# Attention with its scores in a ring of three pairs of PSUM banks and its spread reciprocals in SBUF

## The chip, the core and the metric

The kernel runs on one core of a Trainium2 chip. The core has five engines that work side by side and meet through semaphores: TensorE (PE in the profile, its weight loads PEld), VectorE (DVE), ScalarE (ACT), GpSimd (POOL) and SyncE (SP, which issues most of the DMAs here). The metric is the device time of one execution in microseconds; the median of several executions is compared.

## What is computed

The program is two layers of a MetaFormer on x of 8 images, 128 channels, 32 by 32 pixels. Layer 0 is an attention mixer followed by a spectral mixer; layer 1 is a deformable convolution followed by a mixture of eight experts. The change lies in the attention alone:

```
xp = transpose(ln(x), (0, 2, 3, 1))                  # b, h, w, c
q, k, v = (xp @ w.T).reshape(b, h, w, 8, 16)         # 8 heads of 16 channels
weights = einsum('bhwnd,bxynd->bnhwxy', q, k) / 4
weights = softmax(weights, axis=-1)                  # over y: groups of 32 keys
attn = einsum('bnhwxy,bxynd->bhwnd', weights, v)
x = x + transpose(attn.reshape(b, h, w, c), (0, 3, 1, 2))
```

The softmax runs over the last axis only. A query pixel therefore has 32 separate softmaxes per head, one for each row x of keys, each over 32 keys, and the 32 weighted sums are added.

## The kernel before

All numbers are float32. The attention that runs is `attention_bounded` (the other branch is taken only for inputs whose scores could overflow). It works in **rounds**. An image has 1024 tokens. A **unit** is one block of 256 queries (`QU`, index `qc`) and one half of the heads (`hg`, four heads), so an image has 8 units and the eight images have 64. A unit takes four rounds `r`, and each round covers two of the eight tiles of 128 keys (`c`), for four heads `j`: 256 rounds in all.

- `scores` (L596) makes 8 matmuls into the tile `s` of four PSUM banks, with four heads in four row tiles of 32 rows of the PE array; each head has its 16 channels there and 16 rows of zeros. Then ACT takes one exponential of 2048 elements per partition into `e` in SBUF (L609). `s` has one buffer.
- `add_tiles` (L615): POOL adds the two key tiles of `e` into `t` (L618), 1024 elements per partition from two inputs in SBUF.
- `sums` (L621): PE adds groups of four partitions of `t` into `z`; with the layout of the keys that completes the 32 keys of a softmax. All four rounds of a unit are summed in one round.
- `reciprocals` (L630): DVE takes the reciprocal of `z` out of PSUM into `r`.
- `spread_out` (L634): PE spreads `r` back over the partitions into `rb`, two PSUM banks.
- `divide` (L644): DVE multiplies `e` by `rb` in place (L646), 2048 elements per partition; one input is in SBUF, the other, `rb`, in PSUM.
- `values` (L650): PE multiplies `e` with the values into `av`, one bank, over both halves of the heads.
- `take` and `results` (L664, L668): ACT copies `av` to `o`, PE turns it round with the selection matrix `pick` (L673), which also puts the channels in order, ACT copies it to `at`, and POOL adds it to the image's tokens `xt`.

In between lie the projections for the next image: `keys` (L569) once for each half of the heads and half of the tokens, `queries` (L555), `key_values` (L582), the transposes `tokens` and `channels`, and the layer norm in small pieces on DVE (`bn_stats`, `bn_aggr`), POOL (a row of short operations on 8 elements, L87 to L99) and ACT.

PSUM has eight banks. Before the change four are `s`, two `rb`, one `av`, and one (`small_bank`) is shared by `z` and all projections.

Every engine executes its instructions in program order. That order is written out by hand: `at(round, order, step)` collects all steps, and they are issued sorted by round and by the order within it, with semaphores where tiles are shared. In round R the scores of round R come first (order 0), then POOL's add (1), then `values` of an older unit (2), `spread_out` (2.5), one `divide` (3), `sums` (4), `reciprocals` (5), and the projections (5.5, 6). `e` has 11 buffers, so that it may live from its exponential to its `values`.

Of the kernel before, what the change touches and what calls it, by code (L numbers as in the profile page):

```python
# [11 lines left out]
F32 = mybir.dt.float32  # L12
I32 = mybir.dt.int32
AF = mybir.ActivationFunctionType
ALU = mybir.AluOpType
AX = mybir.AxisListType
PSUM = bass.MemoryType.PSUM

P = 128
B = 8  # L20
C = 128
# [378 lines left out]
class BoundedAttention:  # L400
# [6 lines left out]
    def __init__(self, nc, cp):  # L407
        self.nc = nc
        HG, NH = self.HG, self.NH
        self.xc = cp.tile([P, T], F32, name="xc")  # L410
        self.ht = cp.tile([P, NT, C], F32, name="ht")
        self.hk = cp.tile([P, T], F32, name="hk")
        self.wq, self.wk = (cp.tile([P, HG, NH, 32], F32, name=n) for n in ("wq", "wk"))
        self.wv = cp.tile([C, C], F32, name="wv")
        self.group = cp.tile([P, NG], F32, name="group")
        self.spread = cp.tile([P, 2, P], F32, name="spread")
        self.pick = cp.tile([P, HG, NH, HD], F32, name="pick")

    def keys_view(self):
        return self.hk.rearrange("c (r p) -> c r p", p=P)  # L420
# [34 lines left out]

    def matrices(self, wqT, wkT, wvT):
        nc, HG, NH = self.nc, self.HG, self.NH
        for w, src in ((self.wk, wkT), (self.wq, wqT)):
            nc.gpsimd.memset(w, 0.0)
            for hg in range(HG):  # L460
                nc.sync.dma_start(
                    w[:, hg, :, 0:HD],
                    src[:, hg * NH * HD : (hg + 1) * NH * HD].rearrange("c (h d) -> c h d", d=HD),
                )
        nc.sync.dma_start(self.wv, wvT)

        group = self.group
        nc.gpsimd.memset(group, 1.0)
        nc.gpsimd.affine_select(
            out=group, in_=group, pattern=[[-4, NG]], base=0, channel_multiplier=1,  # L470
            compare_op=ALU.is_ge, fill=0.0,
        )
        nc.gpsimd.affine_select(
            out=group, in_=group, pattern=[[4, NG]], base=3, channel_multiplier=-1,
            compare_op=ALU.is_ge, fill=0.0,
        )

        nc.gpsimd.memset(self.spread, 0.0)
        for j in range(NH):
            part = self.spread[32 * j : 32 * j + 32, j % 2, :].rearrange("p (g m) -> p g m", m=4)  # L480
            nc.gpsimd.affine_select(
                out=part, in_=part, pattern=[[-1, NG], [0, 4]], base=0, channel_multiplier=1,
                compare_op=ALU.not_equal, fill=1.0,
            )


        nc.gpsimd.memset(self.pick, 0.0)
        for hg in range(HG):
            nc.gpsimd.affine_select(
                out=self.pick[:, hg], in_=self.pick[:, hg], pattern=[[-32, NH], [-1, HD]],  # L490
                base=-HD * hg, channel_multiplier=1, compare_op=ALU.not_equal, fill=1.0,
            )


def attention_bounded(ctx, tc, ident, x, x1d, given, weigh, head):


# [8 lines left out]
    QU = 256  # L506
    QC = T // QU
    UNITS = HG * QC
    wq, wk, wv = given.wq, given.wk, given.wv
    group, spread, pick = given.group, given.spread, given.pick  # L510
    hk = given.keys_view()
    cp = ctx.enter_context(tc.tile_pool(name="a_const", bufs=1))
    sb = ctx.enter_context(tc.tile_pool(name="a_sb", bufs=2))
    ep = ctx.enter_context(tc.tile_pool(name="a_e", bufs=11))
    sp = ctx.enter_context(tc.tile_pool(name="a_s", bufs=1, space=PSUM))
    rp = ctx.enter_context(tc.tile_pool(name="a_r", bufs=1, space=PSUM))


# [47 lines left out]
            pq.rearrange("p (r g m) -> p r g m", r=4, m=4),  # L566
        )

    def keys(img, hg, par):  # L569
        if "k" not in img:  # L570
            img["k"] = sb.tile([P, HG, NT, P], F32, tag="k", name="k")
        pk = small_bank("pk")
        nc.tensor.matmul(  # L573
            pk, wk[:, hg].rearrange("c h d -> c (h d)"),
            hk[:, 4 * par : 4 * par + 4, :].rearrange("c r p -> c (r p)"),
            start=True, stop=True,
        )
        nc.scalar.copy(
            img["k"][:, hg, 4 * par : 4 * par + 4, :].rearrange("p c n -> p (c n)"), pk
        )  # L580

    def key_values(b, img, par):  # L582
# [13 lines left out]
    def scores(img, un, r):  # L596

        qc, hg = un["at"]
        s = sp.tile([P, NH, 2, QU], F32, tag="s", name="s")
        q = img["q"][:, hg].rearrange("p a t -> p (a t)")  # L600
        for c in range(2):
            for j in range(NH):
                rows = slice(32 * j, 32 * j + 32)
                nc.tensor.matmul(  # L604
                    s[:, j, c, :], img["k"][rows, hg, 2 * r + c, :],
                    q[rows, qc * QU : (qc + 1) * QU], start=True, stop=True,
                )
        e = ep.tile([P, NH, 2, QU], F32, tag="e", name="e")
        nc.scalar.activation(  # L609
            e.rearrange("p j c q -> p (j c q)"), s.rearrange("p j c q -> p (j c q)"), AF.Exp,  # L610
            scale=float(HD) ** -0.5,
        )
        un["e", r] = e

    def add_tiles(un, r):  # L615
# [16 lines left out]
        nc.vector.reciprocal(un["r"], un["z"][:, 0:QU])  # L632

    def spread_out(un):  # L634
        un["rb"] = rp.tile([P, NH, QU], F32, tag="rb", name="rb")
        for h in range(2):
            for pr in range(2):
                rows = slice(64 * pr, 64 * pr + 64)
                nc.tensor.matmul(  # L639
                    un["rb"][:, 2 * pr + h, :], spread[rows, h, :], un["r"][rows, :],  # L640
                    start=True, stop=True,
                )

    def divide(un, r):  # L644
        e = un["e", r]
# [22 lines left out]
    def results(b, img, qc, qrt):  # L668
        if qc == 0:
            img["at"] = sb.tile([P, NT, C], F32, tag="at", name="at", bufs=1)  # L670
        po = small_bank("po")
        for i in range(2):
            nc.tensor.matmul(  # L673
                po[:, i * P : (i + 1) * P], qrt["o"][:, i * P : (i + 1) * P],
                pick.rearrange("p g j d -> p (g j d)"), start=True, stop=True,
            )
        nc.scalar.copy(
            img["at"][:, 2 * qc : 2 * qc + 2, :].rearrange("p i c -> p (i c)"), po[:, 0 : 2 * P]
        )
        mine = [img[n][:, 2 * qc : 2 * qc + 2, :] for n in ("xt", "at")]  # L680
        nc.gpsimd.tensor_add(mine[0], mine[0], mine[1])
        if qc == QC - 1:
            nc.sync.dma_start(x1d[b], img["xt"])
# [4 lines left out]
    def at(round_no, order, do, *args):  # L688
        work.append((round_no, order, len(work), do, args))
# [5 lines left out]
    for b in range(B):  # L695
        img = {}
        first = 4 * UNITS * b
        project = [
            (keys, img, 0, 0), (keys, img, 0, 1), (queries, img, 0, 0),
            (keys, img, 1, 0), (keys, img, 1, 1), (queries, img, 1, 0),  # L700
            (key_values, b, img, 0), (key_values, b, img, 1),
            (queries, img, 0, 1), (queries, img, 1, 1),
        ]
        if b == 0:
            turn = {"tokens": (0, 0)}
            project_at = (-1, -1, -1, 0, 1, 2, 3, 4, 7, 11)
        else:
            project_at = [first + n for n in (-13, -12, -9, -5, -4, -1, 3, 4, 7, 11)]
            turn = {"channels": (first - 20, first - 17)}
            if b == 1:  # L710
                turn.update(load=0, tokens=(2, 3))
                norm_at = (3, 3, 4, 4, 5, 5, 6, 6) + (6, 7, 7, 8, 8, 8, 9, 9, 9) + (
                    10, 10, 10, 11, 13, 13, 14, 14)
            else:
                turn.update(load=first - 42, tokens=(first - 38, first - 34))
                norm_at = [first - n for n in (
                    37, 36, 35, 34, 33, 32, 32, 31, *range(31, 22, -1), 22, 22, 22, 21, 19, 19, 18, 18
                )]
# [13 lines left out]
        for qc in range(QC):  # L732
            qrt = {}
            for hg in range(HG):
                un = {"at": (qc, hg)}
                t0 = first + 4 * (HG * qc + hg)
                for r in range(4):
                    at(t0 + r, 0, scores, img, un, r)
                    at(t0 + r, 1, add_tiles, un, r)
                    at(t0 + 5, 4, sums, un, r)  # L740
                    at(t0 + 6 + r, 3, divide, un, r)
                at(t0 + 8, 2, values, img, un, 0, (0, 1), qrt)
                at(t0 + 8, 6.5, values, img, un, 1, (0,), qrt)
                at(t0 + 9, 2, values, img, un, 1, (1,), qrt)
                at(t0 + 10, 2, values, img, un, 2, (0, 1), qrt)
                at(t0 + 11, 2, values, img, un, 3, (0, 1), qrt)
                at(t0 + 5, 5, reciprocals, un)
                at(t0 + 6, 2.5, spread_out, un)
            at(t0 + 11, 5, take, qrt)
            at(t0 + 12, 6, results, b, img, qc, qrt)  # L750
    end = 4 * UNITS * B
    spread_rounds(head.pieces(), (end - 40, *range(end - 30, end)))
    with tc.manual_schedule(engines=None):
# [1486 lines left out]
```

## Time and profile before

| | us |
|---|---|
| median of 3 runs | 1885.28 (1880.29 to 1889.61) |
| the profiled execution, its own time | 1886.46 |
| its span, first to last instruction | 1884.7 |
| first exponential of the attention starts | 32.3 |
| last exponential ends | 888.7 |
| granted TensorE clock, whole span / 102 to 850 us / 896 to 1884 us | 0.959 / 1.00 / 0.92 |

| engine | busy in the span, us | busy from 102 to 850 us (748 us), us |
|---|---|---|
| PE | 1682.4 | 742.61 |
| DVE | 1389.0 | 618.25 |
| POOL | 1157.9 | 576.73 |
| ACT | 1064.8 | 507.68 |

The stretch from 102 to 850 us is the attention in its steady course; 225 of the 256 rounds start their exponential in it. A group row of the profile gives the line, the engine, the operation, output and inputs by the program's names, the shapes, the number of instructions, then their busy time and the mean duration in ns, and last the idle time of the engine just before them with what ended it. In a timeline the first number is the start and the second the duration, in us. A PE that is busy all the time is not necessarily at its peak, since matmuls overlap.

### The profile page before, as it was taken

Reading aid. Unit: us, or ns where it says so; the run is one execution under the profiler, and the core shown is the slowest. Engines: PE = TensorE matmul, PEld = TensorE weight load, DVE = VectorE, ACT = ScalarE, POOL = GpSimd, SP = SyncE. Lnnn points to the kernel's source line nnn. Section 1 sums busy time; section 2 is a strip of 40 time slices with the busy share of each in tenths; the row PEclk is TensorE's granted clock in tenths of the full one; section 3 lists DMA queues with packets and bytes.
Section 4 is the critical chain, followed back from the end, with each engine's and each line's share of the span. In section 5 each row is a group of like instructions: output and inputs, shape, how many; then the busy total and the mean of one; then the engine's idle time right before and its main releaser. Section 6 shows DMA issues by size and latency. Waiting matters only on the chain.

```text
span 1884.7 us, 51873 instructions
## 1 busy us (share of the span) xinstructions
PE 1682.4 (89%) x22324; PEld 1033.1 (55%) x22324; DVE 1389.0 (74%) x2107; ACT 1064.8 (56%) x1692; POOL 1157.9 (61%) x1219
## 2 busy tenths in 40 slices
PE   6899999999999999998577899999888497888788
PEld 3455555555555555554233688888665264555555
DVE  3688787878888888888544666666148888999883
ACT  3666666676766667666234455555145655666630
POOL 3778777777878777787221244345126768888740
PEclk9999999999999999999788999999899687999999
DMA  1000000000000000000658322122568775755620
GB/s 30 13 2 24 2 2 24 2 24 2 24 2 24 2 2 24 2 13 2 143 142 242 129 71 71 48 71 59 179 194 263 237 213 153 234 174 164 205 81 21
DMA packets 157998, 156.15 MB, mean 83 GB/s; under 512 B 15424, under 2 KB 136864, under 8 KB 156352
## 3 DMA queue, kind: packets, MB, share of 16 engines
q1 hardware_dynamic: 142400, 102.41, 19.1%
q0 software_dynamic: 15360, 50.34, 8.5%
q8 instruction: 176, 2.88, 0.6%
q14 instruction: 62, 0.51, 0.1%
HBM read 96.39 MB, written 56.33 MB: 81 GB/s over the span
## 4 chain that ended last, share of the span: by engine, by line
PE 60%; DVE 16%; issue 7%; POOL 6%; ACT 4%; DMA 2%; SPq 2%; DVEq 0%; ACTq 0%; POOLq 0%
PE s L604 14%; PE av L656 13%; PE p_g L1958 6%; PE z L625 6%; PE p_z L2007 5%; PE rb L639 4%; PE p_out L1420 3%; DVE ga L1410 3%; DVE g L1317 2%; ACT e L609 2%; PE pq L559 2%; PE pk L573 2%; POOL g L1295 1%; DVE zs L2019 1%; PE po L673 1%
## 5 line engine op out<-in xcount | busy, mean ns | idle before, releaser
L618 POOL TENSOR_TENSOR t<-e 128x1024 f32<-128x1024 f32 x256 | 608.2, 2376 | 204.7 <-ACT e L609 204.4
L646 DVE TENSOR_TENSOR e<-e,rb 128x2048 f32<-128x2048 f32 x256 | 570.4, 2278 | 84.5 <-PE rb L639 84.5
L609 ACT ACTIVATE e<-s 128x2048 f32<-128x2048 f32 x256 | 481.0, 1879 | 255.1 <-PE s L604 252.0
L604 PE MATMUL s<-q,k 32*128 32x256 f32 x4096 | 295.2, 402 | 14.6 <-ACT e L609 13.8
L656 PE MATMUL av<-e,vt 128*32 128x256 f32 x4096 | 287.4, 388 | 4.8 <-DVE e L646 3.5
L1295 POOL DMA_INDIRECT g<-tab,idx x192 | 200.3, 1043 | 134.1 <-ACT cn_m L1515 66.8
L604 PEld LDWEIGHTS s<-q,k 32*128 32x128 f32 x4096 | 185.9, 185 | 137.8 <-ACT e L609 116.9
L1302 ACT ACTIVATE g<-g,w 128x128 f32<-128x128 f32 x604 | 186.4, 390 | 57.0 <-DMA g<-tab,idx 43.2
L1983 POOL TENSOR_SCALAR at<-uc 128x256 f32<-128x256 f32 (+2 forms) x62 | 75.4, 1219 | 173.4 <-PE p_z L2007 128.9
L656 PEld LDWEIGHTS av<-e,vt 128*32 128x32 f32 x4096 | 101.1, 109 | 141.5 <-issue 83.8
L1958 PE MATMUL p_g<-v,a 32*128 32x128 f32 x4096 | 159.3, 284 | 9.4 <-ACT ga L1690 3.7
L632 DVE RECIPROCAL r<-z 128x256 f32<-128x256 f32 x64 | 112.5, 1758 | 70.4 <-PE z L625 70.2
L1958 PEld LDWEIGHTS p_g<-v,a 32*128 32x128 f32 x4096 | 132.3, 186 | 38.3 <-issue 23.0
L1420 PE MATMUL p_out<-ga,ew 128*128 128x512 f32 x256 | 127.5, 645 | 15.5 <-DVE ga L1410 15.4
L625 PE MATMUL z<-t,group 128*32 128x256 f32 x2048 | 122.2, 379 | 0.0
L1692 DVE COPY gb<-p_g 128x512 f32<-128x512 f32 x128 | 82.4, 685 | 46.7 <-PE p_g L1958 46.1
L1692 DVE COPY ga<-p_g 128x512 f32<-128x512 f32 x128 | 82.4, 686 | 44.0 <-PE p_g L1958 44.0
L1690 ACT COPY gb<-p_g 128x512 f32<-128x512 f32 x128 | 68.7, 589 | 69.6 <-PE p_g L1958 68.8
L1690 ACT COPY ga<-p_g 128x512 f32<-128x512 f32 x128 | 68.7, 589 | 66.7 <-PE p_g L1958 66.7
L1410 DVE TENSOR_TENSOR ga<-p_g,tc 128x2048 f32<-128x2048 f32 x32 | 73.0, 2282 | 29.5 <-PE p_g L1401 29.5
L1420 PEld LDWEIGHTS p_out<-ga,ew 128*128 128x128 f32 x256 | 50.1, 205 | 75.6 <-issue 56.2
L625 PEld LDWEIGHTS z<-t,group 128*32 128x32 f32 x2048 | 66.4, 110 | 44.1 <-issue 0.3
(312 smaller groups left out, 2421.3 us busy)
## 6 DMA issues: line engine op xcount, KB each, us to landing
tab<-hx SPq DMA_DIRECT2D x24, 512.0 KB, 5.8
tab<-hx SPq DMA_DIRECT2D x72, 128.0 KB, 5.3
ud<-us SPq DMA_DIRECT2D x8, 1024.0 KB, 5.3
uc<-ud SPq DMA_DIRECT2D x16, 512.0 KB, 4.0
yd<-zs SPq DMA_DIRECT2D x32, 256.0 KB, 3.2
ga<-yd SPq DMA_DIRECT2D x32, 256.0 KB, 3.8
xc<-in_x SPq DMA_DIRECT2D x8, 512.0 KB, 3.9
x1d<-xt SPq DMA_DIRECT2D x8, 512.0 KB, 2.9
```

The source lines that it names most:

```text
L604: nc.tensor.matmul(s[:, j, c, :], img["k"][rows, hg, 2 * r + c, :], q[rows, qc * QU : (qc + 1) * QU], start=True, stop=True,)
L609: nc.scalar.activation(e.rearrange("p j c q -> p (j c q)"), s.rearrange("p j c q -> p (j c q)"), AF.Exp, scale=float(HD) ** -0.5,)
L618: nc.gpsimd.tensor_add(t, e[:, :, 0, :], e[:, :, 1, :])
L625: nc.tensor.matmul(un["z"][32 * j : 32 * j + 32, 0:QU], group, un["t", r][:, j, :], start=(r == 0), stop=(r == 3), skip_group_check=True,)
L646: nc.vector.tensor_tensor(e, e, un["rb"].unsqueeze(2).to_broadcast([P, NH, 2, QU]), ALU.mult)
L656: nc.tensor.matmul(qrt["av"][32 * j : 32 * j + 32, 0:QU], img["v"][:, 2 * r + c, P * hg + 32 * j : P * hg + 32 * j + 32], un["e", r][:, j, ...
L1295: nc.gpsimd.indirect_dma_start(out=t["g", i][:, tap].rearrange("p k c -> p (k c)"), out_offset=None, in_=rows, in_offset=bass.IndirectOffs ...
L1302: nc.scalar.activation(t["g", i][:, tap, k, :], t["g", i][:, tap, k, :], AF.Identity, scale=t["w"][:, i, tap, k : k + 1],)
L1420: nc.tensor.matmul(t["out"], self.ew[:, first + e, :], xg[:, e, :], start=(first + e == 0), stop=(first + e == NE - 1), skip_group_check=True,
L1690: self.nc.scalar.copy(dst, src)
L1692: self.nc.vector.tensor_copy(dst, src)
L1958: nc.tensor.matmul(banks[j][:, i * P : (i + 1) * P], self.a[rows, 4 * n + i, :], self.v[rows, ch].rearrange("p f k -> p (f k)"), start=Tru ...
```

## The change

There are five edits.

1. **Ring.** The score tile becomes two tiles of two banks each, out of a pool of three such pairs. A round takes two pairs; the exponential becomes two instructions of 1024 elements, one for each pair.
2. **Spread reciprocals.** `rb` no longer has banks of its own. `spread_out` writes into a pair of the ring, ACT copies that to a new SBUF tile `rbs`, and `divide` reads both of its inputs, `e` and `rb`, from SBUF. PSUM is then six banks of ring, one of `av`, one shared.
3. **Keys.** Two heads share a row tile of keys: rows 0 to 15 and 16 to 31 of a row tile hold the keys of heads 2j and 2j+1, and the queries have zeros in the rows of the other head. `keys` runs once per half of the tokens, not once per half of the heads too. The weight tiles are loaded accordingly: one DMA for `wk`, two each for `wq` and `wv`, five as before.
4. **Results.** The heads come out in the order of the channels, so `pick` goes and its matmul becomes a transpose.
5. **Order.** `divide`, `values` and `take` come one round later, `results` two rounds later, and the projections follow the shorter list.

```diff
         self.hk = cp.tile([P, T], F32, name="hk")
-        self.wq, self.wk = (cp.tile([P, HG, NH, 32], F32, name=n) for n in ("wq", "wk"))
-        self.wv = cp.tile([C, C], F32, name="wv")
+        self.wq = cp.tile([P, HG, NH, 32], F32, name="wq")
+        self.wk = cp.tile([C, C], F32, name="wk")
+        self.wv = cp.tile([C, HG, NH, HD], F32, name="wv")
         self.group = cp.tile([P, NG], F32, name="group")
         self.spread = cp.tile([P, 2, P], F32, name="spread")
-        self.pick = cp.tile([P, HG, NH, HD], F32, name="pick")
...
         nc, HG, NH = self.nc, self.HG, self.NH
-        for w, src in ((self.wk, wkT), (self.wq, wqT)):
-            nc.gpsimd.memset(w, 0.0)
-            for hg in range(HG):
-                nc.sync.dma_start(
-                    w[:, hg, :, 0:HD],
-                    src[:, hg * NH * HD : (hg + 1) * NH * HD].rearrange("c (h d) -> c h d", d=HD),
-                )
-        nc.sync.dma_start(self.wv, wvT)
+        nc.sync.dma_start(self.wk, wkT)
+        nc.gpsimd.memset(self.wq, 0.0)
+        for hg in range(HG):
+            at = slice(HD * hg, HD * hg + HD)
+            nc.sync.dma_start(
+                self.wq[:, hg, :, at], wqT.rearrange("c (h n) -> c h n", n=2 * HD)[:, :, at]
+            )
+            nc.sync.dma_start(
+                self.wv[:, hg], wvT.rearrange("c (h n) -> c h n", n=2 * HD)[:, :, at]
+            )
...
-        nc.gpsimd.memset(self.pick, 0.0)
-        for hg in range(HG):
-            nc.gpsimd.affine_select(
-                out=self.pick[:, hg], in_=self.pick[:, hg], pattern=[[-32, NH], [-1, HD]],
-                base=-HD * hg, channel_multiplier=1, compare_op=ALU.not_equal, fill=1.0,
-            )
-
-
 def attention_bounded(ctx, tc, ident, x, x1d, given, weigh, head):
...
     UNITS = HG * QC
-    wq, wk, wv = given.wq, given.wk, given.wv
-    group, spread, pick = given.group, given.spread, given.pick
+    wq, wk, wv = given.wq, given.wk, given.wv.rearrange("c g j d -> c (g j d)")
+    group, spread = given.group, given.spread
     hk = given.keys_view()
...
     ep = ctx.enter_context(tc.tile_pool(name="a_e", bufs=11))
-    sp = ctx.enter_context(tc.tile_pool(name="a_s", bufs=1, space=PSUM))
+    sp = ctx.enter_context(tc.tile_pool(name="a_s", bufs=3, space=PSUM))
     rp = ctx.enter_context(tc.tile_pool(name="a_r", bufs=1, space=PSUM))
...
-    def keys(img, hg, par):
+    def keys(img, par):
         if "k" not in img:
-            img["k"] = sb.tile([P, HG, NT, P], F32, tag="k", name="k")
+            img["k"] = sb.tile([P, NT, P], F32, tag="k", name="k")
         pk = small_bank("pk")
         nc.tensor.matmul(
-            pk, wk[:, hg].rearrange("c h d -> c (h d)"),
-            hk[:, 4 * par : 4 * par + 4, :].rearrange("c r p -> c (r p)"),
+            pk, wk, hk[:, 4 * par : 4 * par + 4, :].rearrange("c r p -> c (r p)"),
             start=True, stop=True,
...
         nc.scalar.copy(
-            img["k"][:, hg, 4 * par : 4 * par + 4, :].rearrange("p c n -> p (c n)"), pk
+            img["k"][:, 4 * par : 4 * par + 4, :].rearrange("p c n -> p (c n)"), pk
         )
...
         qc, hg = un["at"]
-        s = sp.tile([P, NH, 2, QU], F32, tag="s", name="s")
+        s = [sp.tile([P, 2, 2, QU], F32, tag="s", name="s") for _ in range(2)]
         q = img["q"][:, hg].rearrange("p a t -> p (a t)")
...
                 nc.tensor.matmul(
-                    s[:, j, c, :], img["k"][rows, hg, 2 * r + c, :],
+                    s[j // 2][:, j % 2, c, :], img["k"][rows, 2 * r + c, :],
                     q[rows, qc * QU : (qc + 1) * QU], start=True, stop=True,
...
         e = ep.tile([P, NH, 2, QU], F32, tag="e", name="e")
-        nc.scalar.activation(
-            e.rearrange("p j c q -> p (j c q)"), s.rearrange("p j c q -> p (j c q)"), AF.Exp,
-            scale=float(HD) ** -0.5,
-        )
+        for h in range(2):
+            nc.scalar.activation(
+                e[:, 2 * h : 2 * h + 2].rearrange("p j c q -> p (j c q)"),
+                s[h].rearrange("p j c q -> p (j c q)"), AF.Exp, scale=float(HD) ** -0.5,
+            )
         un["e", r] = e
...
     def spread_out(un):
-        un["rb"] = rp.tile([P, NH, QU], F32, tag="rb", name="rb")
+        rb = sp.tile([P, 2, 2, QU], F32, tag="s", name="rb")
         for h in range(2):
...
                 nc.tensor.matmul(
-                    un["rb"][:, 2 * pr + h, :], spread[rows, h, :], un["r"][rows, :],
-                    start=True, stop=True,
-                )
+                    rb[:, pr, h, :], spread[rows, h, :], un["r"][rows, :], start=True, stop=True,
+                )
+        un["rb"] = sb.tile([P, NH, QU], F32, tag="rbs", name="rbs")
+        nc.scalar.copy(
+            un["rb"].rearrange("p j q -> p (j q)"), rb.rearrange("p a h q -> p (a h q)")
+        )
...
         for i in range(2):
-            nc.tensor.matmul(
-                po[:, i * P : (i + 1) * P], qrt["o"][:, i * P : (i + 1) * P],
-                pick.rearrange("p g j d -> p (g j d)"), start=True, stop=True,
+            nc.tensor.transpose(
+                po[:, i * P : (i + 1) * P], qrt["o"][:, i * P : (i + 1) * P], ident
             )
...
         project = [
-            (keys, img, 0, 0), (keys, img, 0, 1), (queries, img, 0, 0),
-            (keys, img, 1, 0), (keys, img, 1, 1), (queries, img, 1, 0),
+            (keys, img, 0), (keys, img, 1), (queries, img, 0, 0), (queries, img, 1, 0),
             (key_values, b, img, 0), (key_values, b, img, 1),
...
             turn = {"tokens": (0, 0)}
-            project_at = (-1, -1, -1, 0, 1, 2, 3, 4, 7, 11)
+            project_at = (-1, -1, -1, 2, 3, 4, 7, 11)
         else:
-            project_at = [first + n for n in (-13, -12, -9, -5, -4, -1, 3, 4, 7, 11)]
+            project_at = [first + n for n in (-13, -12, -9, -1, 3, 4, 7, 11)]
             turn = {"channels": (first - 20, first - 17)}
...
                     at(t0 + 5, 4, sums, un, r)
-                    at(t0 + 6 + r, 3, divide, un, r)
-                at(t0 + 8, 2, values, img, un, 0, (0, 1), qrt)
-                at(t0 + 8, 6.5, values, img, un, 1, (0,), qrt)
-                at(t0 + 9, 2, values, img, un, 1, (1,), qrt)
-                at(t0 + 10, 2, values, img, un, 2, (0, 1), qrt)
-                at(t0 + 11, 2, values, img, un, 3, (0, 1), qrt)
+                    at(t0 + 7 + r, 3, divide, un, r)
+                at(t0 + 9, 2, values, img, un, 0, (0, 1), qrt)
+                at(t0 + 9, 6.5, values, img, un, 1, (0,), qrt)
+                at(t0 + 10, 2, values, img, un, 1, (1,), qrt)
+                at(t0 + 11, 2, values, img, un, 2, (0, 1), qrt)
+                at(t0 + 12, 2, values, img, un, 3, (0, 1), qrt)
                 at(t0 + 5, 5, reciprocals, un)
                 at(t0 + 6, 2.5, spread_out, un)
-            at(t0 + 11, 5, take, qrt)
-            at(t0 + 12, 6, results, b, img, qc, qrt)
+            at(t0 + 12, 5, take, qrt)
+            at(t0 + 14, 6, results, b, img, qc, qrt)
     end = 4 * UNITS * B
...
     with tc.manual_schedule(engines=None):
...
```

## The prediction

> **What bounds the kernel now.** I read the page first, for the share of each engine, then the attention's steady stretch, 102 to 850 us, in the table of windows, the groups and the chain. The page's groups for the attention:
>
> ```profile
> L618 POOL TENSOR_TENSOR t<-e 128x1024 f32<-128x1024 f32 x256 | 608.2, 2376 | 204.7 <-ACT e L609 204.4
> L646 DVE TENSOR_TENSOR e<-e,rb 128x2048 f32<-128x2048 f32 x256 | 570.4, 2278 | 84.5 <-PE rb L639 84.5
> L609 ACT ACTIVATE e<-s 128x2048 f32<-128x2048 f32 x256 | 481.0, 1879 | 255.1 <-PE s L604 252.0
> ```
>
> Each of the three runs once a round. The stretch holds 225 exponentials in 748 us, so a round takes 3.324 us and a unit of four 13.30 us; 748 us are 56.25 units. No engine of the three needs that long. The chain of waits over the stretch names the one that does:
>
> ```profile
> by line: PE s L604 33.0%; PE av L656 29.9%; PE z L625 12.9%; PE rb L639 8.0%; PE pq L559 4.0%; PE pk L573 4.0%; PE po L673 2.4%; ACT e L609 2.3%; PE pv L585 2.0%; PE pt L539 1.1%; PE pb L547 0.5%; issue 0.1%
> ```
>
> All but 2.4% is PE. The exponential lies on it with 2.3%: the places where PE is ready for the next scores before `s` is free. Per unit the engines are busy (the stretch's sums over 56.25): PE 13.2 us, DVE 618.25/56.25 = 11.0, POOL 576.73/56.25 = 10.3, ACT 507.68/56.25 = 9.0. DVE and POOL together would need 21.3 us; they fit in 13.3 only because they overlap. Whether they still can is the question that decides here.
>
> [...] `divide` reads `e` from SBUF and `rb` from PSUM, and in the stretch its 226 executions, nearly all beside a POOL addition, hardly vary (minimum, median, maximum in ns):
>
> ```profile
> L646 DVE TENSOR_TENSOR e<-e,rb x226: 2252/2280/2291, 102.2 to 849.4; 128x2048 f32<-128x2048 f32 x113
> ```
>
> Layer 1 has DVE instructions with both inputs in SBUF. L1317 takes 0.95 us as a rule. Once (first two rows) POOL's addition starts 0.07 us before it, once (last two) DVE is first by 0.16 us:
>
> ```profile
> 1428.95 2.37 POOL L1221 TENSOR_TENSOR tok<-tok,cb 128x1024 f32<-128x1024 f32 x1
> 1429.02 3.13 DVE L1317 TENSOR_TENSOR g<-g 128x768 f32<-128x768 f32 x1
> ...
> 1458.01 0.94 DVE L1317 TENSOR_TENSOR g<-g 128x768 f32<-128x768 f32 x1
> 1458.17 3.00 POOL L1221 TENSOR_TENSOR tok<-tok,cb 128x1024 f32<-128x1024 f32 x1 [2.44 <-DVE ht L1076]
> ```
>
> In the first case POOL ends at 1431.32 and DVE at 1432.15: DVE did 0.83 of its 0.95 us after POOL's end, so 0.12 overlapped. In the second DVE ends at 1458.95, POOL at 1461.17: 2.22 of its 2.37 us came after, so 0.15 overlapped. That is full exclusion, with only the start of an instruction hidden.
>
> [...] I keep 2.278 us for its own work (no row of before shows the SBUF form at this size; the 0.95 us of 768 elements plus 1280 elements at the slope 2278/2048 gives 2.37, the other end).
>
> **The change part by part**, per unit unless said.
>
> *Ring.* The exponential becomes two of 1024. No row shows that size; between the ACT copy of 512 from PSUM (587 ns) and the exponential of 2048 (1879) a line gives 1.018 us. ACT: 4 x (2 x 1.018 - 1.879) = +0.63. In exchange the scores of the next round start after half an exponential or none: the 2.3% leave PE's chain, 17.2/56.25 = 0.31 us. Bounds: 0 to 0.31. Order and waits of PE are otherwise the same.
>
> *Spread through the ring.* ACT copies 1024 elements from PSUM: +1.02, taken between exponentials (bounds 0.6 to 1.9 by the two rows above). `divide` now waits for PE's L639, then that copy, some 0.1 us more for the hop; behind it on DVE stands the next reciprocal. This is why edit 5 delays `divide` by a round, and one `divide` of another unit lies between the reciprocal and the first `divide` that needs it.
>
> *Keys.* Two of the four `keys` per image go: half of 4.0% of 748 us is 15.0/56.25 = 0.27 us of PE, and 2 x 0.587/8 = 0.15 of ACT.
>
> *Results.* 4 fp32 matmul records at a time for `po`; a transpose of the same size shows one record per call (`pt`: four for four), so half: 1.2% of 748, 9.0/56.25 = 0.16 us of PE.
>
> *Order and loading.* At the end nothing fills the added round; I add one copy and hops, 2 us in all. Five DMAs before, five after, on SP, all before the first projection; the selection's three short POOL instructions go in the same opening, hidden behind the weights' test. SP's and POOL's queues are otherwise unmoved: 0, within 2 us either way.
>
> Sums without contention: PE 13.30 - 0.31 - 0.27 - 0.16 = 12.56; ACT 9.03 + 0.63 + 1.02 - 0.15 = 10.5; DVE 11.0; POOL 10.3. PE would stay the bound, 0.74 us below now.
>
> *Contention.* `divide` now has two inputs in SBUF, and POOL's additions read SBUF. By the measured overlaps one addition and one `divide` need (2.376 - 0.15) + (2.278 - 0.12) = 4.38 us one after the other: 17.5 a unit. POOL's other operations, (576.73 - 534.6)/56.25 = 0.75 (534.6 are the additions of the stretch), read SBUF too. [...] I add 0.4 for handovers that fail (a `divide` that waits for its copy while POOL waits for an exponential): **18.7**.
>
> Additions and `divide` run beside each other in 256 - 7 = 249 rounds, 62.25 units. (18.7 - 13.3) x 62.25 = 336 us, and 2 for the end. Against the profiled execution, 1886.46 (its span 1884.7 and 1.8 around it; 1.2 above the median): 1886.5 + 338 = 2224.5, so **2224 us**.
>
> **The rivals.**
>
> A. *The lock with bad handovers.* If POOL or DVE cannot use what the other leaves, DVE's own 2.2 us add up: 18.3 + 2.2 = 20.5, (20.5 - 13.3) x 62.25 = 448, 2336 us. For it: PE executes in order and blocks in `values` on a late `divide`, which holds up the scores and so POOL's next work. Against: `values` come two rounds after their `divide` and `sums` two after the last addition, so both engines have some two rounds of slack.
>
> B. *No lock in this form: faster.* The place is L646's second input. If a `divide` with `rb` in SBUF overlaps additions as the one with PSUM does, the unit is PE's 12.56 and the time 1886.5 - 0.74 x 64 + 2 = 1841 us. The point from which it decides: the change is even when 18.3 shrinks to 13.3, that is when each `divide` overlaps 1.25 us of its 2.28 with additions instead of about 0.27. For it: nothing in the attention of before shows the SBUF form. Against: the two pairs above.
>
> C. *The lock in part*, or a gain after it: [...]. That could give back some 20 us of 2197 (18.3 without the 0.4): 2177.
>
> **How the numbers follow.** The lock with good or fair handovers (2177 to 2290): 0.77. A or worse: 0.15. Partial exclusion below 2177 but still slower: 0.02. B: 0.05. About even: 0.01. So faster by over 0.5% (about what a measurement of this kernel can tell from no change) 0.05, within it 0.01, slower 0.94. The range takes in the floor with C and reaches to A: 2175 to 2336.
>
> **What would show it.** In the profile after, L646's successor and L618 keep their counts of 256, but their mean durations rise from 2.28 and 2.38 us, each by up to what the other holds (2.2 us), with minima still near the old ones; rounds of about 4.7 us; PE's idle time before `values` on `divide` appears, and PE's share in the stretch falls to about 12.6/18.7 = 67%. Two exponentials a round of about 1.02 us and a copy of 1.02 a unit test ACT's prices. If the divides stay at 2.28 us beside additions, I am wrong and B holds; if they stretch but the round is above 5.1 us, A does.

## The result, and the profile after

The changed kernel takes **2198.89 us** (median of 4 runs, 2194.11 to 2202.78) against 1886.33 us for the kernel before (1880.29 to 1889.61). The ratio is **1.166**, 95% interval 1.162 to 1.170: 313 us slower, where 338 were forecast. The profiled execution took 2202.78 us with a span of 2201.1.

The page's groups for the three operations of a round, and for the new copy:

```profile
L612 POOL TENSOR_TENSOR t<-e 128x1024 f32<-128x1024 f32 x256 | 909.8, 3574 | 53.9 <-ACT e L603 53.1
L643 DVE TENSOR_TENSOR e<-e,rbs 128x2048 f32<-128x2048 f32 x256 | 857.7, 3386 | 37.7 <-ACT rbs L637 31.9
L603 ACT ACTIVATE e<-s 128x1024 f32<-128x1024 f32 x512 | 497.5, 1027 | 400.5 <-PE s L597 338.8
...
L637 ACT COPY rbs<-rb 128x1024 f32<-128x1024 f32 x64 | 65.0, 1015 | 86.7 <-PE rb L633 71.7
```

The counts are the same, 256 each. Neither the addition nor `divide` works on more data than before, but their means are 3.57 and 3.39 us where they were 2.38 and 2.28. At the same time POOL's idle time before the addition has shrunk to 53.9 us. The loss does not appear as waiting. It appears as busy time: an instruction that waits for the other engine's is counted as busy meanwhile, as in the two pairs of layer 1 in the prediction (3.13 us for a DVE instruction of 0.95). The tile `e` from 102 to 850 us shows how the durations spread (minimum, median, maximum in ns):

```profile
L612 POOL TENSOR_TENSOR t<-e x165: 2332/4382/4472, 101.6 to 847.2; 128x1024 f32<-128x1024 f32 x165
L643 DVE TENSOR_TENSOR e<-e,rbs x165: 2227/3635/4470, 102.5 to 849.3; 128x2048 f32<-128x2048 f32 x165
```

The minima lie close to the durations of before. The additions' median is one own duration and one of `divide`, less the overlapped starts: 2.38 + 2.28 - 0.27 = 4.39; no instruction of either kind takes more than 4.47. Two timelines, POOL's and below it DVE's, over the same stretch:

```profile
597.95 30.41 POOL L612 TENSOR_TENSOR t<-e 128x1024 f32<-128x1024 f32 x7 [0.15 <-ACT e L603]
```

```profile
600.28 4.04 DVE L643 TENSOR_TENSOR e<-e,rbs 128x2048 f32<-128x2048 f32 x1
604.28 1.76 DVE L626 RECIPROCAL r<-z 128x256 f32<-128x256 f32 x1
605.95 0.24 DVE L79 BATCH_NORM_STATS2 lp_st<-xt 128x6 f32<-128x128 f32 x1
606.22 0.18 DVE L80 BATCH_NORM_AGGREGATE lp_mv<-lp_st 128x2 f32<-128x6 f32 x1
606.32 2.37 DVE L643 TENSOR_TENSOR e<-e,rbs 128x2048 f32<-128x2048 f32 x1
```

Seven additions take 30.41 us, 4.34 each, with no gap: POOL always has an addition under way, and where a `divide` stands beside it the two take turns. The reciprocal, which reads PSUM, takes 1.76 us beside them, as it did before. And the sums of the stretch from 102 to 850 us:

```profile
102.00:850.00 748.00, 600.71 (x7162) 322.77 (x7158) 639.17 (x286) 414.97 (x515) 728.98 (x270) 0.90 0.03 8
```

After the stretch and its length the columns are PE, PEld, DVE, ACT, POOL, each with its instructions, then PE's clock. PE, busy 742.61 us there before, is down to 600.71, and POOL is up to 728.98 of 748. All of POOL's operations in this stretch read SBUF. I took from the trace the time in which a `divide` or a POOL operation is under way: 745.9 of the 748 us. The two taking turns leave hardly any time free, and that, not PE, sets the pace.

PE's granted clock in this stretch fell from 1.00 to 0.90, and PE's matmuls became longer too (those of the scores 444 ns on average, 400 before). That does not explain the longer additions and `divide`s: in e1 below PE's clock is just as low, 0.91, and they take 2364 and 2267 ns.

I measure a unit in every trace from the start of the 33rd `divide` to that of the 225th, divided by 48: **13.30 us before, 18.27 after**. What follows the last `divide` takes as long as before: it ends at 906.6 of 1884.7 us before and at 1223.5 of 2201.1 after, which leaves 978.1 and 977.6. The whole loss lies in the attention.

### The profile page after: what moved, and what is told of

The parts are those of the page before. It is cut to its first block, busy times and chain, and to the rows that moved or that the text cites. A ratio compares the mean times of both kernels' runs of the same rounds, so it can differ in the third digit from the quotient of the medians.

```text
span 2201.1 us, 52097 instructions
## 1 busy us (share of the span) xinstructions
PE 1783.3 (81%) x22228; PEld 1082.0 (49%) x22228; DVE 1666.8 (76%) x2107; ACT 1127.7 (51%) x1996; POOL 1624.5 (74%) x1215
## 4 chain that ended last, share of the span: by engine, by line
PE 28%; POOL 27%; DVE 23%; issue 12%; ACT 5%; DMA 2%; SPq 1%; DVEq 0%; ACTq 0%; POOLq 0%
POOL t L612 14%; DVE e L643 9%; PE p_g L1953 6%; PE p_z L2002 5%; PE s L597 4%; PE av L653 3%; PE p_out L1415 2%; DVE ga L1405 2%; ACT e L603 2%; POOL xt L677 2%; DVE r L626 2%; DVE g L1312 2%; PE rb L633 1%; PE z L619 1%; POOL lp_y L95 1%
## 5 line engine op out<-in xcount | busy, mean ns | idle before, releaser
L612 POOL TENSOR_TENSOR t<-e 128x1024 f32<-128x1024 f32 x256 | 909.8, 3574 | 53.9 <-ACT e L603 53.1
L643 DVE TENSOR_TENSOR e<-e,rbs 128x2048 f32<-128x2048 f32 x256 | 857.7, 3386 | 37.7 <-ACT rbs L637 31.9
L603 ACT ACTIVATE e<-s 128x1024 f32<-128x1024 f32 x512 | 497.5, 1027 | 400.5 <-PE s L597 338.8
L597 PE MATMUL s<-q,k 32*128 32x256 f32 x4096 | 359.2, 449 | 27.9 <-ACT e L603 27.2
L653 PE MATMUL av<-e,vt 128*32 128x256 f32 x4096 | 314.1, 417 | 20.6 <-DVE e L643 17.5
L597 PEld LDWEIGHTS s<-q,k 32*128 32x128 f32 x4096 | 225.6, 209 | 161.3 <-issue 92.6
L619 PE MATMUL z<-t,group 128*32 128x256 f32 x2048 | 144.4, 409 | 127.0 <-POOL t L612 126.5
L633 PE MATMUL rb<-r,spread 64*128 64x256 f32 x512 | 85.3, 456 | 63.1 <-DVE r L626 40.0
L637 ACT COPY rbs<-rb 128x1024 f32<-128x1024 f32 x64 | 65.0, 1015 | 86.7 <-PE rb L633 71.7
L633 PEld LDWEIGHTS rb<-r,spread 64*128 64x128 f32 x512 | 53.8, 218 | 100.5 <-issue 84.9
```

The source lines that it names most:

```text
L597: nc.tensor.matmul(s[j // 2][:, j % 2, c, :], img["k"][rows, 2 * r + c, :], q[rows, qc * QU : (qc + 1) * QU], start=True, stop=True,)
L603: nc.scalar.activation(e[:, 2 * h : 2 * h + 2].rearrange("p j c q -> p (j c q)"), s[h].rearrange("p j c q -> p (j c q)"), AF.Exp, scale=fl ...
L612: nc.gpsimd.tensor_add(t, e[:, :, 0, :], e[:, :, 1, :])
L619: nc.tensor.matmul(un["z"][32 * j : 32 * j + 32, 0:QU], group, un["t", r][:, j, :], start=(r == 0), stop=(r == 3), skip_group_check=True,)
L633: nc.tensor.matmul(rb[:, pr, h, :], spread[rows, h, :], un["r"][rows, :], start=True, stop=True,)
L643: nc.vector.tensor_tensor(e, e, un["rb"].unsqueeze(2).to_broadcast([P, NH, 2, QU]), ALU.mult)
```

## The experiments

Two theories stood against each other. **Exclusion**: `divide` with two SBUF inputs and POOL's reads take turns. **Structure**: the ring, the two exponentials, the copy or the later order cost the time. e1, e5, e2, e8 and e9 ran on chips where the kernel before takes 1935 to 1937 instead of 1886 us. Their traces have 1026 to 1028 us after the last `divide`, where before and after have 978. That is the whole difference, so I take the attention to be as fast there (no trace of before was taken on these chips), and ratios and units are compared, not times.

| kernel | ratio to before (95%) | unit, us | mean `divide`, ns | mean addition, ns |
|---|---|---|---|---|
| before | 1 | 13.30 | 2278 | 2376 |
| after | 1.166 (1.162 to 1.170) | 18.27 | 3386 | 3574 |
| e1_rb_in_psum | 1.116 (1.112 to 1.120) | 17.02 | 2267 | 2364 |
| e5_keys_and_results | 0.995 (0.993 to 0.998) | 13.17 | 2278 | 2377 |
| e2_copy_alone | 1.186 (1.183 to 1.190) | 18.96 | 3374 | 3189 |
| e8_psum_old_order | 0.993 (0.991 to 0.996) | 13.07 | 2277 | 2375 |
| e3_no_additions | 1.054 (1.049 to 1.058) | 14.94 | 2323 | none |
| e4_pool_writes | 1.021 (1.017 to 1.025) | 13.82 | 2321 | 952 (memset) |
| e6_half_additions | 1.067 (1.063 to 1.071) | 15.00 | 3009 | 3327 (128) |
| e7_old_order | 1.189 (1.184 to 1.195) | 18.86 | 3317 | 3245 |
| e9_no_pool_reads | 0.993 (0.991 to 0.996) | 13.21 | 2272 | 953 (memset) |

**e1_rb_in_psum.** The kernel after, with `rb` in PSUM again.

```diff
-    sp = ctx.enter_context(tc.tile_pool(name="a_s", bufs=3, space=PSUM))
+    sp = ctx.enter_context(tc.tile_pool(name="a_s", bufs=2, space=PSUM))
-        rb = sp.tile([P, 2, 2, QU], F32, tag="s", name="rb")
+        rb = rp.tile([P, 2, 2, QU], F32, tag="rb", name="rb")
-        un["rb"] = sb.tile([P, NH, QU], F32, tag="rbs", name="rbs")
-        nc.scalar.copy(...)
+        un["rb"] = rb.rearrange("p a h q -> p (a h) q")
```

> The kernel after with edit 2 undone alone: the spread reciprocals stay in two PSUM banks of their own, ACT's copy is gone, divide reads one input from SBUF and one from PSUM; the ring then has two pairs, not three. Exclusion theory: divide and the additions overlap again, both at 2.28 and 2.38 us, PE is the bound with about 12.6 to 13.0 us a unit, 1840 to 1870 us. Rival, the ring with two exponentials or the later order of divide and values makes the loss: still above 2150 us.

Measured: 1.116, or about 2105 us where before takes 1886, far from the 1840 to 1870 us that I expected. Yet `divide` is back at 2267 ns and the addition at 2364:

```profile
L640 DVE TENSOR_TENSOR e<-e,rb 128x2048 f32<-128x2048 f32 x175 | 391.4, 2267 | 69.6 <-PE rb L633 61.0 <-POOL t L612 4.0 <-PE po L667 2.5
```

So the stretching is gone, and a new wait took its place. The kernel's waits from 102 to 850 us (total, times, longest, in us):

```profile
PEld rb L633 <- DVE e L640: 112.6, 44, 2.9
PE rb L633 <- DVE e L640: 91.4, 44, 2.4
```

The step I had missed: `rb` has one buffer in PSUM here (`bufs=1`). With `divide` a round later, the last `divide` of a unit stands in the same round as the next unit's `spread_out`, and behind it in order. PE then waits for DVE before it may overwrite `rb`, and DVE waits for PE before it may go on. With edit 2 undone the stretching goes, but this kernel cannot serve as the change without edit 2: edit 5 needs the second buffer that `rbs` has in SBUF.

**e8_psum_old_order.** The same, with edit 5 undone too.

```diff
-                    at(t0 + 7 + r, 3, divide, un, r)
+                    at(t0 + 6 + r, 3, divide, un, r)
-                at(t0 + 9, 2, values, img, un, 0, (0, 1), qrt)
+                at(t0 + 8, 2, values, img, un, 0, (0, 1), qrt)
...
```

> As the first kernel of this call (edit 2 undone, ring of two pairs), with edit 5 undone too: divide and values in the rounds of before. Exclusion theory: within 10 us of that kernel, 1840 to 1870 us, since neither order leaves PE waiting. If the later order matters by itself, the two differ by more.

Measured: 0.993, a unit of 13.07 us. By itself the ring of two pairs with two exponentials, the shared keys and the transpose cost nothing; they gain 0.7%, most of which (0.5%) the keys and the transpose have without the ring, in e5. This version is faster than both kernels. Against e1 the old order is worth 3.95 us a unit, so that part of the expectation (within 10 us of e1) failed. The wait just shown is 91.4/44 = 2.1 us of it. Most of the rest is time in which PE is busy: as many matmuls in a unit take 14.7 us in e1 (645.67 of 748 us busy) and 13.0 in e8 (744.89), at a granted clock of 0.91 and 1.00.

**e5_keys_and_results** and **e2_copy_alone.** Edits 3 and 4 on the kernel before; then the copy to SBUF on top, nothing else:

```diff
-        un["rb"] = rb.rearrange("p a h q -> p (a h) q")
+        un["rb"] = sb.tile([P, NH, QU], F32, tag="rbs", name="rbs")
+        nc.scalar.copy(
+            un["rb"].rearrange("p j q -> p (j q)"), rb.rearrange("p a h q -> p (a h q)")
+        )
```

> Edits 3 and 4 alone (keys of two heads in one row tile, transpose in place of the selection) on the kernel before. Both theories: PE loses 0.27 + 0.16 us a unit, 28 us in all, about 1858 us; it is the base of the next kernel.

> Edits 3 and 4, and on top ACT's copy of the spread reciprocals to SBUF alone: score tile of four banks, one exponential a round and the order of before. Exclusion theory: an addition and a divide take turns, 18.25 us a unit, about 2200 us, as the whole change. Rival, the loss comes from the ring, the two exponentials or the order: below 1880 us.

Measured: 0.995 and 1.186. The copy to SBUF, added alone, carries the whole loss, and a little more; score tile, exponential and order are those of before. So the ring, the two exponentials and the later order are out as the cause; whether it is the copy itself or what `divide` then reads, the next kernels tell, which all keep the copy. e5 itself gained 0.5%, not 1.5%: most of the 0.43 us a unit that PE was to save turned into waiting for `s`. In e5's chain from 102 to 850 us the exponential has 12.9% where it had 2.3%, and the wait of PE's matmuls for it, 4.4 us before, is

```profile
PE s L597 <- ACT e L602: 17.1, 24, 1.1
```

**e3_no_additions**, **e4_pool_writes**, **e6_half_additions.** Here `rb` stays in SBUF, copied by ACT as in the change, and the other party changes. e4 leaves out the sums over the keys.

```diff
 # e3 (all r) and e6 (r = 1, 3): no t; z sums both key tiles of e
+                src = un["t", r][:, j, :] if c is None else un["e", r][:, j, c, :]
 # e4
-        nc.gpsimd.tensor_add(t, e[:, :, 0, :], e[:, :, 1, :])
+        for _ in range(2):
+            nc.gpsimd.memset(t, 1.0)
```

> The kernel after, rb in SBUF as it is, without POOL's additions: PE sums both key tiles of e itself, 32 more records for z a unit (12.9% of 748 us is 1.72 us a unit). Exclusion theory: [...] PE is the bound at 12.56 + 1.72 = 14.3 us a unit, about 1950 us. Rival, divide is slow because of SBUF, the copy or its place: divide stays above 3 us and the time above 2100 us.

> The kernel after with each of POOL's additions replaced by two memsets of t to 1.0 (two writes of 1024 elements, no reads); so the sums over the keys are left out. By the memsets of before (952 ns for 1024 elements) POOL is busy 1.9 us a round beside divide. Exclusion of reads alone: divide at 2.28 us, PE the bound, 1840 to 1870 us. Rival, any POOL instruction excludes such a divide: 4 x (1.9 + 2.16) + 0.75 = 17.0 us a unit, about 2120 us.

> The kernel after with POOL's additions in rounds 0 and 2 of a unit only; in rounds 1 and 3 PE sums both key tiles itself. Exclusion theory: [...] PE needs 12.56 + 0.86 = 13.4; 13.8 to 14.4, about 1920 to 1960 us, and divide at about 3 us on average. Rival, the loss does not come from the additions: above 2150 us.

The rows of `divide` from 102 to 850 us, first e3's, then e4's:

```profile
L649 DVE TENSOR_TENSOR e<-e,rbs 128x2048 f32<-128x2048 f32 x200 | 458.4, 2323 | 18.8 <-ACT rbs L643 18.3
L644 DVE TENSOR_TENSOR e<-e,rbs 128x2048 f32<-128x2048 f32 x218 | 499.4, 2321 | 19.5 <-ACT rbs L638 19.0
```

Without the additions `divide` falls to 2323 ns, still with two SBUF inputs: it is not slow because of SBUF or the copy. With the same engine busy beside it in memsets it falls to 2321 ns, while the memsets keep the 952 ns they had before. So POOL's writes do not hold up `divide`; its additions, which read SBUF, do (3386 ns in the kernel after). With half of the additions `divide` takes 3.0 us on average, as expected, and the loss is about a third, by the units: 15.00 - 13.30 = 1.70 us of 4.97.

All three are slower than I expected. For e4 the groups of POOL from 102 to 850 us show why:

```profile
L613 POOL MEMSET t<- 128x1024 f32 x433 | 404.9, 952 | 88.1 <-PE z L620 75.4
L678 POOL TENSOR_TENSOR xt<-xt,at 128x256 f32<-128x256 f32 x27 | 41.0, 1519 | 66.8 <-ACT at L674 66.8
L95 POOL TENSOR_TENSOR lp_y<-lp_y,lp_w 128x8 f32<-128x8 f32 x18 | 23.7, 1319 | 0.0
...
L89 POOL TENSOR_SCALAR lp_v<-lp_v 128x8 f32<-128x8 f32 x6 | 13.7, 2277 | 0.0
```

L89 works on 8 elements and took 238 ns in the same stretch before; here it takes 2277 on average, as long as if it first waited for nearly a whole `divide`. The memsets, and with them the sums, queue behind such waits on POOL. In e6 DVE comes close to being the bound: in the stretch it is busy 697.73 of 748 us, `divide`'s waits for half the additions included.

**e9_no_pool_reads.** e4, with the layer norm's short operations and the last addition moved from POOL to DVE (`nc.gpsimd` to `nc.vector`), so that POOL reads nothing beside `divide` in the stretch over which the unit is measured. (16 short reads for the next mixer's layer norm remain beside the last units, from 811 to 841 us.) The sums over the keys are left out as in e4.

> The kernel with two memsets in place of POOL's additions (so without the sums over the keys), and now also the short operations of the attention's layer norm and the final addition to the tokens moved from POOL to DVE: POOL reads nothing from SBUF beside divide. Exclusion theory: what made the memset kernel 2.1% slower than before were POOL's short reads of 0.2 us, each waiting up to a whole divide (2.3 us) with the memsets, and so sums, queued behind it; without them 1840 to 1870 us. Rival, the ring of three pairs, ACT's copy or the later order cost something by themselves: still above 1900 us.

Measured: 0.993, 1923.19 beside 1937.44 us, which is about 1873 us where before takes 1886: just outside the range I gave, far below the rival's. The unit falls from 13.82 to 13.21, and `divide` to

```profile
L646 DVE TENSOR_TENSOR e<-e,rbs 128x2048 f32<-128x2048 f32 x227 | 510.7, 2272 | 7.1 <-ACT rbs L640 7.1
```

that is, 2272 ns with both inputs in SBUF, as fast as before with one in PSUM (2278). It also fits e3: 13.21 and the 1.72 us of extra sums are 14.93, and 14.94 was measured. That is a sum and no test, since e3 keeps POOL's short reads and e9 does not.

**e7_old_order.** The kernel after with edit 5 undone.

> The kernel after with edit 5 undone alone: divide, values and take one round earlier, results two. Exclusion theory: [...] 18.2 to 18.6 us a unit, 2195 to 2225 us. Rival, handovers: with one round less of slack divide waits for its copy while POOL has nothing to add, up to 20.5 us a unit and 2330 us.

Measured: 1.189, 2244.35 us, a unit of 18.86. That lies between the two expectations, 20 us above the first's range and far from the second's end; 8 of these 20 us lie after the last `divide` (986.1 against 977.6 us), and why is open. The waits from 102 to 850 us show what comes in:

```profile
ACT rbs L637 <- PE rb L633: 136.8, 40, 5.6
DVE e L643 <- ACT rbs L637: 123.8, 40, 4.5
POOL t L612 <- ACT e L603: 104.9, 43, 5.9
```

DVE waits for its copy 40 times, about once a unit, and POOL waits for exponentials for 104.9 us where it waited 17.2 in the kernel after. In these moments both can be without work: of 748 us neither a `divide` nor a POOL operation is under way for 18.9, or 0.5 us a unit, against 2.1 us in all in the kernel after. That is what rival A is about, at 0.6 us a unit. e2, in the old order as well, has 18.96 and 22.9 us of such time. So edit 5 gives back what edit 2 would cost on top of the exclusion.

## Why the prediction was right

**Right: the bound and its price.** From two pairs of instructions in layer 1 I took 2.22 and 2.16 us for an addition and a `divide` that take turns, which makes 17.5 a unit, 0.75 for POOL's other reads, and 18.3 us in all. That the other reads count as well was an estimate, which no pair of before showed; L89 and e9 bear it out. The unit is 18.27, and a `divide` or a POOL operation is under way for 745.9 of 748 us, as this bound requires. That price and measurement agree to 0.03 us is in part luck: seven additions without a gap took 4.34 each, not 4.38, which makes 17.4 + 0.75 = 18.1. (18.27 - 13.30) x 62.25 = 309 us, with 2 for the end 311; the profiled execution is 316 longer, since the loss fell on nearly all 64 units.

**Mis-sized: the handovers.** I added 0.4 us a unit for handovers that fail. At most 2.1 us of 748, or 0.05 us a unit, were lost to them here. 0.4 x 62.25 = 25 us is more than the distance between the 338 us forecast and the 316 between the two profiled executions; without the allowance the forecast would have been 313. I had argued that two rounds of slack keep both engines supplied; that was right, and the allowance contradicted it. e7 shows the same term at 0.6 with one round less. Rival A at its full 2.2 us (per unit of before 1.76 for DVE's reciprocal and 0.45 for `bn_stats` and `bn_aggr`) did not occur in either.

**Right: what the parts cost elsewhere.** The exponential of 1024 takes 1.027 us and the copy 1.015, against 1.018 for both; the SBUF form of `divide`, for which I had kept 2.278 us as an estimate, took 2272 ns in e9.

**Wrong: PE's share.** I expected it to fall to about 67% in the stretch; it fell to 80%, 600.71 of 748 us. I had counted PE's work at the speed of before, and its matmuls became longer at the lower granted clock (13.0 us a unit busy in e8 at 1.00, 14.7 here at 0.90). PE was still not the bound, so the time did not suffer.

**Wrong, with no effect on the forecast: rival B's time.** I took 12.56 us for a unit without contention. e9 needs 13.21 with the ring, copy and order of the change (and DVE's extra work), e8 13.07 with `rb` in PSUM. PE's savings came in full in e8, whose chain has 95.7% of PE, 12.5 us of 13.07; what I had put at nothing are the waits, the other 0.56 us, of which the exponential still has 1.7% of the chain. e5 shows one of them growing: PE becomes ready earlier and waits for `s`. What fills the rest of e9's 13.21 I have not isolated. By e8 and e9 a version without contention gains about 0.7%, not 2.4%. The point at which the change would be even is wrong as well: 18.3 shrinks to 13.3 when each `divide` overlaps 1.25 us more than the 0.27 assumed, so 1.52 us.

**Rival C** did not show, and its 20 us were an estimate of mine that no trace of before had shown: the additions and `divide`s excluded each other in full (4.34 us for the pair, as above), and the part after the attention took 977.6 us against 978.1, at a granted clock of 0.92 in both. (Its 2197 us leave out the 2 us for the end.)

## What to carry to other kernels

Before an operand of a VectorE instruction is moved from PSUM to SBUF to free banks, look at the instruction's other input and at what GpSimd does at that time: where both inputs then lay in SBUF and GpSimd read SBUF too, the two engines' durations had to be added here, not laid side by side (4.34 us for an addition of 2.38 and a `divide` of 2.28). The instruction's duration without such a neighbour gave no warning (2272 ns, against 2278 with `rb` in PSUM). In a profile, look for durations that spread with equal shapes from one value to nearly its double (2332 to 4472 ns for the addition here), on an engine that seems busy and never idle. Where an operand has to go to SBUF, take away GpSimd's reads, short ones included, because an operation of 8 elements waited here as long as one of 1024: about 2.0 us for both here (L89, 2277 ns instead of 238, and the additions' median, 4.38 us instead of 2.38).

## What the runs showed of the hardware that I had not expected

GpSimd's operations of 0.2 us waited for nearly all of a `divide` (L89: 238 ns before, 2277 in e4; in the kernel after one of L87 lasts from 628.44 to 630.60 us, beside a `divide` that ends at 630.51) and held up what was queued behind them; with the last addition's reads that cost 0.6 us a unit (13.82 against 13.21 when both are taken off GpSimd). TensorE's mean granted clock from 102 to 850 us was 0.88 to 0.91 in the four kernels where it was busy 584 to 646 of 748 us (after, e1, e2, e7), and 0.99 to 1.00 in the seven where it was busy 694 us or more. These are means over one stretch of one program; what sets the clock no run shows.
